# Re-ordering three row-square additions and one small product in a hand-scheduled graph-network kernel

## Chip, cores and metric

The kernel runs on one core of a Trainium2 chip (trn2). The metric is device time in microseconds (us) for the whole launch: median, lowest and highest of three runs. One further execution was taken with the hardware profiler; all durations quoted from "the trace" come from that one. Engines are named as the profile names them: PE (TensorE; PEld is its weight load), DVE (VectorE), ACT (ScalarE), POOL (GpSimd), SP (the engine whose queue issues the DMAs).

## What is computed

Sixteen graphs (batches) of 1024 nodes with 128 features each and a dense weighted adjacency matrix `adj` of 1024 x 1024 float32 values. Cut to what matters, the reference is:

```python
def gnn0(x, adj):                       # first block
    deg = adj.sum(-1)[:, :, None]
    s = einsum('bid,bij->bjd', x, adj) / deg
    return relu(concat([x, s], -1) @ W.T + b)

def layer(nodes, adj):                  # second block, four of these
    src = nodes @ ws + bs
    src_agg = einsum('bjv,bij->biv', src, adj / l2norm_of_rows(adj))
    dst = nodes @ wd + bd
    dst_agg = einsum('bjv,bji->biv', dst, adj / l2norm_of_columns(adj))
    own = nodes @ wn + bn
    return tanh(concat([src_agg, own, dst_agg], 2) @ wu + bu)

x = layernorm(x + gnn0(x, adj))
x = layernorm(x + four_layers(x, adj))  # layers 2 and 3 also take earlier outputs as input
```

The two norms of `adj` need, for each batch, the sum of the squares of every row and of every column. Those sums, and one of the two layer norms, are what the change touches.

## The kernel before

**Tiling.** One pass of the loop `for b in range(B)` does the four layers (0 to 3) of batch b and, in between, everything that batch n = b + 1 needs before its own layers: loading `adj`, its row and column norms, scaling, the first block, and its layer norm. `a` is batch b's matrix scaled by columns (128 partitions, 8 blocks of 1024), `at` its transpose scaled by rows. `a2` (`w["a"]` while it is fresh) is the matrix of batch n. The second norm of batch b - 1 is finished during layers 1 and 2 of batch b.

**Matrix products.** Each layer's aggregation is a Strassen-like scheme of seven products of half-size blocks, for each of the two directions (DST, with `a`; SRC, with `at`). It needs sums of quarters of the matrices: `T` for `a` and `Q` for `at`; `combine(i, y, T)` (lines 674 to 682) writes quarter sum i with one DVE instruction over 128 x 2048 elements. Every product has 64 output rows, so PE works on two at once, an "upper" one on output partitions 64 to 127 and a "lower" one on 0 to 63. `aggregate` lists the upper and lower products; `in_turn` interleaves them and numbers the upper ones. One such *step* is one upper and one lower product of 64 x 512, which the trace shows as two PE records each.

**What sets the order.** Nothing is left to a scheduler: all engines run exactly in the order in which the Python code issues. `aggregate` carries two dictionaries from step number to function. `events` are the layer's own reads of finished products, `hooks` are other work to be issued ahead of that step; at one step, events come first. PE's instructions of a hook therefore stand in PE's queue at that step, while DVE's and ACT's instructions just join their own queues at that place.

**Layer 0, steps and reads (batches 1 to 15).** Upper: Z1, Z0 own terms (steps 0, 1), M1 DST (2 to 5), M2 DST (6 to 9), M1 SRC (10 to 13), Z21 DST (14 to 17), M2 SRC (18 to 21, reads `Q[2]`), M3 SRC (22 to 25, reads `Q[3]`), Z21 SRC (26 to 29, reads `Q[4]`). The reads that matter here:

- before step 14, `m1_read` (L884, L885): two ACT copies;
- before step 22, `m2_and_half_of_m3`: DVE add L892, ACT copy L893, DVE add L910; then `m4_read`: ACT copies L888, L889;
- before step 26, `last_reads`: DVE adds L896 (the read of M3) and L901, ACT copy L897, DVE add L902, then the tanh L1018 on ACT that writes the upper half (columns 512 to 1023) of `f1T`;
- after the last step: DVE add L1007 (`e0 + Z0`) and the tanh L1018 of the other half of `f1T`.

Layer 1 then begins with `messages` (L247 products `pt`, which read `f1T`: first the upper half, 16 PE records, then the lower half, 16 more), whose results DVE adds at L698, followed by the sums L710 to L713.

**Row and column squares of batch n.** `squares_of_row(n, a, st, i)` is an ACT Square of row block i into a tile `sq` (line 322), which also yields the row sums. `add_squares` adds those tiles up on DVE into `acc`: line 329 for the first pair, line 331 for the others. The `sq` tiles come from a pool of two buffers, so the Square of row block 2 waits until the first addition has freed a buffer. Row blocks 0 to 3 are done in layer 0, 4 to 7 in layer 1; then `column_sums` (L339, L344) reduces `acc`, and `inverses` (L368 to L376) ends with a power of -1/2 on POOL (L376). These hooks exist in the passes b = 1 to 14; b = 0 has its own arrangement, and b = 15 has no next batch.

**The norm in layer 1.** `begin1` (step 2), `centre1` (16), `squares1` (19) and `rstd1` form the second layer norm of batch b - 1. `squares1` is the DVE reduction L446, which writes `v`. `rstd1` calls `norm_rstd`: a product of `v` with a constant matrix on PE (L252, tile `pv`, four small records), a DVE scaling of it (L454, tile `ve`) and a power on POOL (L456, tile `rs`). `norm_end` (L461) uses `rs` in layer 2.

The hooks before the change, layer 0 first:

```python
hooks = {0: rows3, 3: weights1, 5: lambda: combine_1(yt), 7: lambda: combine(2, yt, Q),
         9: lambda: combine(3, yt, Q), 11: lambda: combine(4, yt, Q), 15: sums1, 20: additions(1),
         22: additions(then=(2, 3)), 27: additions(2, 3)}
...
hooks = alongside(sums_of_next, {2: begin1, 16: centre1, 19: squares1, 23: rstd1})
```

`additions(*which, then)` issues the DVE additions of `which` and then the ACT Squares of `then`; `sums1` issues the Squares of row blocks 0 and 1.

Of the kernel before, what the change touches and what calls it, by code (L numbers as in the profile page):

```python
# [23 lines left out]
def adj_resnorm_kernel(ctx: ExitStack, tc: tile.TileContext, x, adj, w0, b0, layers, out):  # L24
# [308 lines left out]
    def column_sums(b, state):  # L333

        column_reduce(b, state, column_transpose(b, state))
# [326 lines left out]
    def quarters(a):  # L662
        return {(j, h): a[:, j * NJ:(j + 1) * NJ, half(h)] for j in range(2) for h in range(NH)}
# [4 lines left out]
    def combined(b, kind):  # L668

        return {i: one.tile([P, NJ, HW], F32, tag=f"{kind}{i}", name=f"{kind}{i}_{b}") for i in (2, 3, 4)}  # L670
# [5 lines left out]
    def combine(i, y, T):  # L676
        if i == 2:
            nc.vector.tensor_sub(T[2], y[1, 1], y[0, 1])  # L678
        elif i == 3:
            nc.vector.tensor_sub(T[3], T[2], y[0, 0])  # L680
        else:
            nc.vector.tensor_sub(T[4], y[1, 0], T[2])
# [342 lines left out]
    def alongside(hooks, more):  # L1025

        def both(i):
            def run():
                hooks[i]()
                more[i]()  # L1030
            return run

        return hooks | {i: both(i) if i in hooks else f for i, f in more.items()}
# [36 lines left out]
    Q = combined(0, "Q")  # L1070
# [166 lines left out]
    for b in range(B):  # L1237
        nxt = b + 1 < B
        n = b + 1
        y, yt = quarters(a), quarters_t(at)  # L1240
# [5 lines left out]
        if b == 0:  # L1246
            def row_factors0():
                nonlocal rinv
                rinv = gather_inverses(0, row_inverses(0, inv))
                column_sums(0, st0)  # L1250
                for q in (2, 3):
                    scale_rows(rows[q], q, rinv)

            t = messages(b, 0, feats, wm, {0: lambda: to_x1(0), 2: row_factors0}, with_sums=False)
            cinv = {}

            def columns0(rows, h, engine=nc.vector):
                scale_columns(a, cinv[0], rows, half(h), engine)

            def rows0(destination, finish):  # L1260
                for q in (2, 3):
                    transpose_rows(rows[q], q, at)

            def cinv0(destination, finish):
                cinv[0] = factor_rows_now(0, 1, inv, "cinv")

            def second0(destination, finish):
                columns0(range(NJ, NB), 1)
                sums_of_weights(2, fetched[2][3])
                weight_sums(own_seven(2, fetched[2][3]))  # L1270
                nc.sync.dma_start(wsave[2], fetched[2][3])
                destination(1, cinv[0])
                columns0(range(NJ), 1)

            def fold_and_scale(l, q):
                fold_begin(l, fetched[l])
                scale_rows(rows[q], q, rinv)

            def first0(destination, finish):
                columns0(range(NJ, NB), 0, nc.gpsimd)  # L1280
                columns0(range(2), 0, nc.gpsimd)
                for q in (0, 1):
                    transpose_rows(rows[q], q, at)
                destination(0, cinv[0])
                columns0(range(2, NJ), 0)

            def sums0(destination, finish):
                combine_1(y)
                finish(1)
                combine(2, y, T)  # L1290
                combine_1(yt)
                combine(3, y, T)

            def folded(l, part):
                return lambda *_: part(l, fetched[l])

            hooks = {4: lambda *_: inverses(0, st0, NB), 5: folded(2, fold_begin), 6: rows0, 7: cinv0,
                     8: folded(2, fold_end), 9: lambda *_: fold_and_scale(3, 0), 11: second0, 12: folded(3, fold_end),
                     14: lambda *_: scale_rows(rows[1], 1, rinv), 18: first0, 26: sums0}
            T = combined(0, "T")  # L1300
            plain_layer(b, 0, feats, t, wm, a, at, f1, "acc", hooks)
            wm = message_weights(b, 1)
            a2 = load(n)
            xs2 = load_spread(n)
        else:
            w = {}
            if nxt:
                st = begin_sums(n)
            t = messages(b, 0, feats, wm)
            if nxt:  # L1310
                w["a"] = load(n)
            Q = combined(b, "Q")
            ahead = {}

            def weights1(ahead=ahead):
                combine(4, y, T)
                ahead["wm"] = message_weights(b, 1)

            def rows3():
                transpose_rows(rows[0], 0, at)  # L1320

            def sums1(w=w, st=st):
                if nxt:
                    for i in range(2):
                        squares_of_row(n, w["a"], st, i)

            def additions(*which, then=(), w=w, st=st):
                def issue():
                    if nxt:
                        for i in which:  # L1330
                            add_squares(n, st, i)
                        for i in then:
                            squares_of_row(n, w["a"], st, i)
                return issue

            hooks = {0: rows3, 3: weights1, 5: lambda: combine_1(yt), 7: lambda: combine(2, yt, Q),
                     9: lambda: combine(3, yt, Q), 11: lambda: combine(4, yt, Q), 15: sums1, 20: additions(1),
                     22: additions(then=(2, 3)), 27: additions(2, 3)}
            aggregate(b, 0, feats, t, wm, a, at, T, Q, f1, "row", hooks)
            wm = ahead["wm"]  # L1340
            a2, xs2 = w.get("a"), None
# [21 lines left out]
        hooks = {}  # L1363
        if b == 0:
            hooks = {0: sums_of(0, 1, add=(1,)), 1: lambda: combine(2, yt, Q), 2: sums_of(of=FIRST),
                     3: sums_of(2, 3, add=(2, 3)), 4: lambda: combine(3, yt, Q), 5: sums_of(4, 5, add=(4, 5)),
                     6: lambda: combine(4, y, T), 13: sums_of(6, 7), 18: lambda: combine(4, yt, Q), 19: sums_of(of=LAST),
                     22: sums_of(add=(6, 7)), 27: lambda: column_sums(n, st)}
            st = begin_sums(n)
        else:  # L1370
            nm = f"1_{b - 1}"
            w = {"ys": summed(f"y{nm}", "xa")}
            sums_of_next = {}
            if nxt:
                sums_of_next = {0: sums_of(4, 5), 1: sums_of(of=FIRST, add=(4, 5)), 2: sums_of(6, 7),
                                8: sums_of(add=(6, 7)), 9: lambda: column_sums(n, st), 15: sums_of(of=(4,)),
                                18: sums_of(of=(5,)), 20: lambda: inverses(n, st), 21: sums_of(of=(6,)),
                                24: sums_of(of=(7,))}

            def begin1(w=w, nm=nm):  # L1380
                norm_spread(w["ys"], f4, KS)
                w["s"] = norm_sum(w["ys"], KS, nm, back)

            def centre1(w=w, nm=nm):
                w["sq"] = norm_centre(w["ys"], w["s"], KS, nm)
                if nxt:
                    w["xs"] = load_spread(n)

            def squares1(w=w, nm=nm):
                w["v"] = norm_squares(w["sq"], KS, nm)  # L1390

            def rstd1(w=w, nm=nm):
                w["r"] = norm_rstd(w["v"], KS, nm)

            hooks = alongside(sums_of_next, {2: begin1, 16: centre1, 19: squares1, 23: rstd1})
        hooks = alongside(hooks, {3: weights2})
        p = {}

# [6 lines left out]
        hooks = alongside(hooks, {11: y4, 27: t2})  # L1405
# [49 lines left out]
        hooks, between = {4: end1} if b else {}, {}  # L1455
        if nxt:
            scales = [lambda: scale(0, 1), lambda: scale(NJ, 1), lambda: scale(0, 0), lambda: scale(NJ, 0)]
            if b == 0:
                between = {1: inverses3, 2: factors}
                hooks = {1: load_xn, 5: factors_of_rows, 7: start3, 18: factors_gathered,  # L1460
                         **dict(zip((10, 12, 14, 16), scales))}
                quarters_at = (20, 22, 25)
            else:
                between = {0: factors, 3: end1_and_load}
                hooks = {2: factors_of_rows, **dict(zip((4, 5, 7, 9), scales)), 10: factors_gathered, 16: start3}
# [8 lines left out]
        hooks = alongside(hooks, {23: weights3})  # L1474
        if b == 0:
            hooks = alongside(hooks, {8: lambda: weight_sums(own_seven(3, None))})
# [9 lines left out]
        hooks, between = {}, {}  # L1486
        if nxt:
# [75 lines left out]
            def rows3():  # L1563
# [4 lines left out]
            hooks = {5: rstd0, 7: rows0, 11: quarter0, 15: end0, 8: scale2, 16: scale3, 18: acc_rows, 22: rows1, 23: lambda: scale1(0),  # L1568
                     26: lambda: scale1(1), 27: rows2, 30: rows3}
        else:  # L1570
# [17 lines left out]
            hooks = {30: residual_last, 31: transpose_last}  # L1588
# [66 lines left out]
```

## Time and profile before

| what | value |
|---|---|
| three runs: median (lowest to highest) | 2426.66 us (2425.36 to 2427.37) |
| profiled execution: its own time | 2427.01 us |
| profiled execution: span, first to last instruction | 2425.1 us |
| PE busy | 2384.9 us (98% of the span) |
| DVE busy | 2084.5 us (86%) |
| ACT busy | 977.2 us (40%) |
| POOL busy | 273.5 us (11%) |
| mean granted TensorE clock | 0.998 |
| column-square additions, L329 and L331 together | 105, of 1.22 us each |
| Squares, L322 | 120, of 1.05 us each |

How to read it: the busy share of an engine says how much of the span it had an instruction running. PE matmuls are pipelined and their ends are modelled, so a matmul record of 0.59 us does not mean that PE spends 0.59 us on it; the distance from one start to the next does. A number in square brackets behind a record of the timeline is the idle time of that engine just before it, with the instruction that ended the wait.

### The profile page before, as it was taken

What the parts mean: (1) busy time and instruction counts of PE and PEld (TensorE: products, weight loads), DVE (VectorE), ACT (ScalarE), POOL (GpSimd) and SP (SyncE); (2) the same over time, 40 slices, a digit from 0 to 9 for tenths busy, and PEclk for the clock granted to TensorE, in tenths of its full rate; (3) what the DMA queues carried; (4) which work ended last, traced back from release to release, by engine and by line L of the source; (5) the groups of instructions that cost most, each with busy time, mean ns of one, the idle gap of its engine ahead of it and who ended that gap; (6) DMA issues with size and microseconds to landing.
All of it is one profiled execution on the core that took longest, in us unless ns stands there. A gap on an engine that the chain in (4) does not pass through costs nothing.

```text
span 2425.1 us, 39279 instructions
## 1 busy us (share of the span) xinstructions
PE 2384.9 (98%) x15293; PEld 1213.7 (50%) x15293; DVE 2084.5 (86%) x2799; ACT 977.2 (40%) x1827; POOL 273.5 (11%) x102
## 2 busy tenths in 40 slices
PE   8999999999999999999999999999999999999998
PEld 4444464544645446454554545546454464544644
DVE  5998888988889889889888889888898888988954
ACT  5524344253343524435244452434425334253312
POOL 4101111001111011110111100111100111101100
PEclk9999999999999999999999999999999999999999
DMA  9527244262633627235272442634427253362400
GB/s 205 120 74 145 68 116 86 71 143 56 138 71 82 135 48 160 56 96 114 54 162 52 110 96 66 150 68 105 87 70 154 56 128 79 73 142 50 99 21 21
DMA packets 365896, 232.02 MB, mean 96 GB/s; under 512 B 152784, under 2 KB 336848, under 8 KB 365712
## 3 DMA queue, kind: packets, MB, share of 16 engines
q1 hardware_dynamic: 364944, 227.16, 42.1%
q0 software_dynamic: 768, 2.36, 0.4%
q8 instruction: 121, 1.98, 0.3%
q14 instruction: 63, 0.52, 0.1%
HBM read 209.59 MB, written 19.84 MB: 95 GB/s over the span
## 4 chain that ended last, share of the span: by engine, by line
PE 55%; DVE 26%; ACT 7%; SPq 4%; DMA 4%; issue 4%; DVEq 0%; POOLq 0%; ACTq 0%
PE m L1005 20%; PE z L1005 13%; PE pt L247 6%; PE pt_z L247 5%; PE m_f L583 5%; SPq L640 4%; DVE acc L331 3%; PE z_f L583 2%; PE pw L247 2%; DVE at L655 2%; DVE t L698 2%; DMA rows<-in_adj_dram 2%; ACT a L647 2%; DVE Q L678 1%; DVE Q L680 1%
## 5 line engine op out<-in xcount | busy, mean ns | idle before, releaser
L1005 PE MATMUL m<-a,t 128*64 128x512 f32 x1008 | 432.3, 593 | 0.2 <-DVE t L711 0.2
L1005 PE MATMUL m<-at,t 128*64 128x512 f32 x1008 | 417.0, 592 | 0.0
L1005 PE MATMUL m<-Q,S 128*64 128x512 f32 x880 | 394.0, 593 | 0.0
L1005 PE MATMUL m<-T,S 128*64 128x512 f32 (+1 forms) x1040 | 393.1, 573 | 0.0
L456 POOL TENSOR_TENSOR rs<-ve,mhalf 128x32 f32<-128x32 f32 x30 | 191.6, 6385 | 996.1 <-DVE ve L454 996.1
L1005 PE MATMUL z<-at,t 128*64 128x512 f32 x504 | 232.0, 593 | 0.0
L1005 PE MATMUL z<-at,S 128*64 128x512 f32 x504 | 228.3, 593 | 0.0
L1005 PE MATMUL z<-a,S 128*64 128x512 f32 x504 | 228.2, 593 | 0.0
L1005 PE MATMUL z<-a,t 128*64 128x512 f32 x504 | 226.8, 592 | 0.0
L1005 PE MATMUL z<-Q,t 128*64 128x512 f32 x504 | 226.6, 592 | 0.0
L1005 PEld LDWEIGHTS m<-T,S 128*64 128x64 f32 x1040 | 133.6, 137 | 127.0 <-issue 123.5
L1005 PEld LDWEIGHTS m<-a,t 128*64 128x64 f32 x1008 | 133.2, 137 | 123.9 <-issue 114.0
L1005 PEld LDWEIGHTS m<-at,t 128*64 128x64 f32 x1008 | 134.9, 137 | 113.2 <-issue 110.8
L1005 PEld LDWEIGHTS m<-Q,S 128*64 128x64 f32 x880 | 118.2, 137 | 114.8 <-issue 112.9
L1005 PE MATMUL z<-T,t 128*64 128x512 f32 x384 | 175.7, 593 | 0.0
L884 ACT COPY e<-m 64x512 f32<-64x512 f32 x63 | 36.6, 581 | 335.4 <-PE m L1005 334.9
L376 POOL TENSOR_TENSOR inv<-cols,mhalf 128x16 f32<-128x16 f32 (+1 forms) x17 | 46.8, 2752 | 1050.4 <-DVE cols L375 1050.4
L414 DVE TENSOR_TENSOR a<-a,cinv 128x512 f32<-128x512 f32 x250 | 154.1, 692 | 1.4 <-ACT cinv L351 1.3
L247 PE MATMUL pt<-wm,f1T 128*64 128x128 f32 (+1 forms) x1536 | 124.7, 310 | 14.6 <-ACT f1T L1018 14.6
L322 ACT ACTIVATE sq<-a 128x1024 f32<-128x1024 f32 x120 | 125.8, 1049 | 14.4 <-DVE acc L331 13.4
L247 PEld LDWEIGHTS pt<-wm,f1T 128*64 128x64 f32 x1536 | 94.3, 137 | 63.4 <-ACT f1T L1018 32.2
L317 ACT ACTIVATE a<-a 128x1024 f32<-128x1024 f32 x120 | 125.3, 1045 | 0.4
(300 smaller groups left out, 4922.3 us busy)
## 6 DMA issues: line engine op xcount, KB each, us to landing
a<-in_adj_dram SPq DMA_DIRECT2D x120, 512.0 KB, 12.9
rows<-in_adj_dram SPq DMA_DIRECT2D x480, 64.0 KB, 2.1
a<-in_adj_dram SPq DMA_DIRECT2D x240, 128.0 KB, 3.4
wm<-wsave SPq DMA_DIRECT2D x32, 704.0 KB, 5.3
wm<-wsave SPq DMA_DIRECT2D x31, 320.0 KB, 3.1
xn<-in_x_dram SPq DMA_DIRECT2D x124, 64.0 KB, 5.4
xs<-in_x_dram SPq DMA_DIRECT2D x60, 128.0 KB, 3.6
cinv<-dr SPq DMA_DIRECT2D x30, 256.0 KB, 6.3
```

The costliest lines, as they stand in the source:

```text
L247: nc.tensor.matmul(out[s], x[:, s], y, start=start, stop=stop)
L317: nc.scalar.activation(a[:, i, :], a[:, i, :], AF.Copy, accum_out=degree)
L322: nc.scalar.activation(sq, a[:, i, :], AF.Square, accum_out=state["cols"][:, i:i + 1])
L331: nc.vector.tensor_add(state["acc"], state["acc"], state[i])
L414: engine.tensor_mul(a[:, i, s], a[:, i, s], cinv[:, s])
L456: nc.gpsimd.tensor_tensor(rstd, ve, mhalf[:, :n], ALU.pow)
L583: nc.tensor.matmul(o, x_, y_, start=start, stop=stop)
L640: nc.sync.dma_start(piece[g * C:(g + 1) * C, :, h * P:(h + 1) * P], v[h, g, :, k:k + n])
L647: nc.scalar.activation(row, row, AF.Copy, scale=rinv[:, q * QB + k:q * QB + k + 1])
L655: nc.vector.transpose(at[h][:, j:j + NJ, c].rearrange("p j (k c) -> p j k c", c=C), piece.rearrange("p k (j c) -> p j k c", c=C)[:, j:j + NJ])
L698: nc.vector.tensor_add(t[j][:, o:o + 2].rearrange("p k a v c -> p k (a v c)"), pt, wm[:, 0][:, None, :].to_broadcast([P, 2, 2 * P]))
L1005: nc.tensor.matmul(o, x, y_, start=start, stop=stop)
```

## The change

Only two dictionaries of hooks change. In layer 0 of passes 1 to 14, the first addition of squares is issued at step 16 instead of 20, and the quarter sum `Q[4]` at step 17 instead of 11, so that the addition stands ahead of `Q[4]` in DVE's queue. The Squares of row blocks 2 and 3 are issued at step 18 instead of 22. The addition of row block 2 is issued at step 23 instead of 27; that of row block 3 stays at 27. In layer 1, `rstd1` is issued at step 26 instead of 23 (passes 1 to 15).

```diff
             hooks = {0: rows3, 3: weights1, 5: lambda: combine_1(yt), 7: lambda: combine(2, yt, Q),
-                     9: lambda: combine(3, yt, Q), 11: lambda: combine(4, yt, Q), 15: sums1, 20: additions(1),
-                     22: additions(then=(2, 3)), 27: additions(2, 3)}
+                     9: lambda: combine(3, yt, Q), 15: sums1, 16: additions(1), 17: lambda: combine(4, yt, Q),
+                     18: additions(then=(2, 3)), 23: additions(2), 27: additions(3)}
...
-            hooks = alongside(sums_of_next, {2: begin1, 16: centre1, 19: squares1, 23: rstd1})
+            hooks = alongside(sums_of_next, {2: begin1, 16: centre1, 19: squares1, 26: rstd1})
```

In the order of each engine this gives, for one of those passes: DVE runs L680 (`Q[3]`), L329, L682 (`Q[4]`), L892, L910, L331, L896, L901, L902, L331, L1007, where it ran L680, L682, L329, L892, L910, L896, L901, L902, L331, L331, L1007. ACT runs the four Squares in a row ahead of L893, L888, L889, where the last two Squares stood behind L889. On PE the four small records of `pv` move three steps back. No instruction is added or removed, and the orders on SP and POOL stay the same.

## The prediction, as put on record

> **What bounds the kernel now.** I read the page's busy shares first, then PE's own waits, then the timeline of one pass (b = 2; the others repeat it), then that of the last pass (b = 15).
>
> ```profile
> PE 2384.9 (98%) x15293; PEld 1213.7 (50%) x15293; DVE 2084.5 (86%) x2799; ACT 977.2 (40%) x1827; POOL 273.5 (11%) x102
> ```
>
> PE is the bound, so only a change in PE's idle time can move the end. Who makes PE wait (total us, times, longest):
>
> ```profile
> PE pt L247 <- ACT f1T L1018: 14.6, 14, 1.0
> PE pv L252 <- DVE v L446: 6.9, 14, 0.5
> ```
>
> Two waits recur 14 times, once in each pass that prepares a next batch, and they are the two places that the edit touches. The first, in pass 2:
>
> ```profile
> 377.90 0.69 DVE L910 TENSOR_TENSOR e<-e,e 64x512 f32<-64x512 f32 x1 [0.68 <-ACT e L893]
> 379.78 0.69 DVE L896 TENSOR_TENSOR e<-e,m 64x512 f32<-64x512 f32 x1 [1.19 <-PE m L1005]
> 381.30 0.61 ACT L897 COPY e<-e 64x512 f32<-64x512 f32 x1
> 381.94 0.69 DVE L902 TENSOR_TENSOR e<-e 128x512 f32<-128x512 f32 x1 [0.75 <-ACT e L897]
> 382.55 2.48 DVE L331 TENSOR_TENSOR acc<-acc,sq 128x1024 f32<-128x1024 f32 x2
> 382.67 0.72 ACT L1018 ACTIVATE f1T<-e,bout 128x512 f32<-128x512 f32 x1 [0.76 <-DVE e L902]
> 382.99 0.59 PE L1005 MATMUL z<-at,t 128*64 128x512 f32 x1
> 383.44 1.95 PE L247 MATMUL pt<-wm,f1T 128*64 128x256 f32 x16
> 384.95 0.68 DVE L1007 TENSOR_TENSOR e<-e,z 128x512 f32<-128x512 f32 x1
> 385.66 0.72 ACT L1018 ACTIVATE f1T<-e,bout 128x512 f32<-128x512 f32 x1 [2.27 <-DVE e L1007]
> 386.44 1.95 PE L247 MATMUL pt<-wm,f1T 128*64 128x256 f32 x16 [1.04 <-ACT f1T L1018]
> 388.21 1.03 PE L1005 MATMUL z<-f1T,wm 128*64 128x512 f32 x4
> ```
>
> PE's last product of layer 0 starts at 382.99 and would release L1007 some 0.6 later, but two additions hold DVE until 384.95; L1007, the tanh and the second half of the messages are late by that much. Just before, DVE idles 0.68, 1.19 and 0.75: room for the additions. Pass 15 has no additions and shows the place without them:
>
> ```profile
> 2313.91 0.59 PE L1005 MATMUL z<-at,t 128*64 128x512 f32 x1
> 2313.93 4.06 PE L247 MATMUL pt<-wm,f1T 128*64 128x256 f32 x32
> 2314.54 0.69 DVE L1007 TENSOR_TENSOR e<-e,z 128x512 f32<-128x512 f32 x1 [1.64 <-PE z L1005]
> 2317.82 1.03 PE L1005 MATMUL z<-f1T,wm 128*64 128x512 f32 x4
> ```
>
> The second wait, in layer 1 of pass 2: the small product stands in PE's queue before its operand `v` is there.
>
> ```profile
> 407.48 1.22 DVE L446 TENSOR_REDUCE v<-sq 128x32 f32<-128x1024 f32 x1
> 407.76 0.59 PE L1005 MATMUL z<-T,t 128*64 128x512 f32 x1
> 408.85 0.31 PE L252 MATMUL pv<-v,fold 128*64 128x32 f32 x4 [0.49 <-DVE v L446]
> 408.96 0.62 PE L1005 MATMUL z<-T,t 128*64 128x512 f32 x1
> 411.54 0.18 DVE L454 TENSOR_SCALAR ve<-pv 128x32 f32<-128x32 f32 x1
> ```
>
> [...]L1007 starts at 384.95, right behind the additions, though its operand was ready near 383.6. [...]So I count PE from start to start: a pair of 64 x 512 records takes 0.43 (407.33 to 407.76), not 0.59. [...]in pass 15 the messages start 0.02 after the last lower product, on the free half.
>
> **Part 1, layer 0.** One addition is 1.22 (rows L329, L331), a quarter sum 2.2, a Square 1.05, all moved and none added. Worked through pass 2:
>
> - DVE ends `Q[3]` at 373.16. Squares 0 and 1 are done by 372.8, so the first addition runs 373.16 to 374.4 and `Q[4]` ends at 376.5 instead of 375.3. PE wants `Q[4]` at step 26, 379.58: hidden, 3.0 spare. L892 starts at 376.52 as before.
> - ACT: Squares 2 and 3 get their buffers at 374.4 and run to 376.6 (2 x 1.05 and a 0.19 accumulator read), inside ACT's idle 4.45 ahead of L893. L893 (377.25), L888 and L889 are not delayed. Their rows came with the same four transfers as rows 0 and 1, squared from 370.6 on. Nothing else moves on ACT; SP and POOL have nothing moved past them.
> - Addition 2 follows L910: 378.6 to 379.83, in the 1.19 idle. L896 moves from 379.78 to 379.85: 0.07.
> - L897 no longer stands behind two Squares (it waited until 381.30): it starts at 380.6, when L896 is done. L902 runs 381.2 to 381.9, and the upper `f1T` half is there at 382.65 instead of 383.39. PE can start the messages at 383.01 instead of 383.44.
> - Addition 3: 381.9 to 383.15. L1007 then waits for PE alone: in pass 15 it starts 0.63 after the last product, here 382.99 + 0.63 = 383.62, with 0.45 spare.
>
> From the last product's start to layer 1's own terms, pass 2 takes 388.21 - 382.99 = 5.22 and pass 15 takes 2317.82 - 2313.91 = 3.91. I take the whole difference, **1.31 per pass**; the 1.04 that PE's waits give is the lower end (it counts modelled ends and leaves out the 0.43 at 383.44). What remains of a wait, about 0.35, is the chain L1007, tanh, messages, which pass 15 has too.
>
> DVE behind L1007 follows PE's messages (L698 idled 0.74 for PE), so all of layer 1 comes 1.31 earlier on DVE, ACT and PE alike, `v` included. This part alone would leave the second wait at its size.
>
> **Part 2, layer 1.** From product to product across `pv`, pass 2 takes 408.96 - 407.76 = 1.20; pass 15, where `v` was early, takes 0.52. So the wait is **0.68** (lower end 0.49, the waits' number). Three steps are 3 x 2 x 0.43 = 2.57 of PE work; the wait is covered with about 1.9 spare. The four small records cost the same 0.1 anywhere. Who waits for them now: on DVE L454, ahead of L721. Without the stall step 26 falls at 408.96 - 0.68 - 0.1 + 2.57 = 410.75 in the old frame, `pv` is there at about 411.05, and L454 came at 411.54: still no wait, 0.5 spare; beyond that, L1007 there idled 2.05 for PE. On POOL, L456 starts at 412.39 anyway, because it queues behind L376; L461 reads its result at 427.42. If that cover were gone, each us of delay of L721 beyond 2.05 would hit the messages of layer 2.
>
> **Sum.** 14 x (1.31 + 0.68) = 27.9 us. Against the profiled execution's own 2427.01 (span 2425.1 and 1.9 around it), that is 2399.1; this execution lies 0.35 above the median, so the runs should show about **2399**. With both lower ends, 14 x 1.53 = 21.4: 2405. Next in line is PE itself: the remaining gaps in pass 2 are below 0.1 each but for the 0.35.
>
> **Rivals.**
>
> - *The addition at M3's read becomes the wait.* If addition 2 could only start when M3 is ready (379.78), L896 starts at 381.0, the upper half of `f1T` comes at 383.8, L1007 at 384.4 and the second messages at 385.86 instead of 386.44: gain 0.58 + 0.68, times 14 = 17.6: **2409**. For it: the slots fit within 0.07, and addition 2 needs Square 2. Against: Square 2 is ready 3 us earlier. Chance 0.12.
> - *The small product's wait only changes place*, to L454 and L721 or to layer 2's messages: only 14 x 1.31 = 18.3: **2408**. Against it: the 2.05 that DVE idles at L1007. Chance 0.10.
> - *Slower: the Squares stall ACT ahead of the reads.* If rows 2 and 3 landed only with the last of the eight transfers of the next matrix (the last is issued at 359.5 and lands 19.9 us later, 379.4), Square 2 would start at 379.4 instead of 374.4, L893 at 381.5, and the chain L910, addition 2, L896, L897, L902 would bring the messages' second half to about 388.8: 2.4 later than now, less 0.68, so 14 x 1.7 = 24 us: **2451**. It turns into a loss once Square 2 starts after about 377.7, 3.3 later than I expect. Against it: rows 0 and 1, of the same transfers, are squared at 370.6 without a wait. Chance 0.04.
> - *No change*: the gains are given back at a place that the trace doesn't show as tight. Chance 0.02. That the change doesn't do what it says is excluded by the orders on the engines, which are written out by hand.
>
> **Numbers.** The forecast, 2396 to 2405 by itself, has 0.72. Faster: 0.72 + 0.12 + 0.10 = 0.94; within 0.2% (4.9 us, about what a measurement here tells from no change) 0.02; slower 0.04. The range reaches to 2409 to take in the first two rivals; its low end is the forecast less 3 us for the spread of single executions and for some of the 0.35.
>
> **What would show it.** In the profile after: both rows gone or near zero among PE's waits (I allow 0.3 per pass at the second messages); one addition between L910 and L896 and one ahead of L1007, the latter starting about 0.63 after the last product; 3.9 from that product to layer 1's own terms; L897 right behind L896; `pv` without idle before it. The forecast is wrong if L896 starts well behind M3's end, if ACT idles before Square 2 for a DMA, or if L454 or L721 waits for `pv`.

## The result, and the profile after

| | before | after |
|---|---|---|
| median (lowest to highest), four runs each | 2426.93 us (2425.36 to 2427.37) | 2397.44 us (2397.09 to 2398.95) |
| profiled execution: own time, span | 2427.01, 2425.1 us | 2397.22, 2395.3 us |
| one pass (median distance from one layer 0's last product to the next) | 148.51 us | 146.48 us |
| last product of layer 0 to layer 1's own terms (pass 2) | 5.22 us | 3.91 us |
| product to product across `pv` (pass 2) | 1.20 us | 0.51 us |

The ratio is 0.9881, with a 95% interval of 0.9864 to 0.9898: 1.2% faster. The forecast was 2399.

The page's busy line and the line of the chain that ended last, by engine, of the kernel after:

```profile
PE 2377.4 (99%) x15293; PEld 1195.3 (50%) x15293; DVE 2088.5 (87%) x2799; ACT 977.2 (41%) x1827; POOL 273.8 (11%) x102
...
PE 95%; DVE 2%; DMA 1%; SPq 1%; issue 0%; ACT 0%; POOLq 0%; DVEq 0%; ACTq 0%
```

The same chain line of the kernel before:

```profile
PE 55%; DVE 26%; ACT 7%; SPq 4%; DMA 4%; issue 4%; DVEq 0%; POOLq 0%; ACTq 0%
```

PE's own busy time fell by 7.5 us only, the span by 29.8: the other 22.3 us were idle time of PE. The chain tells it best. Before, two short waits per pass were enough to lead the walk back from PE into the DVE queue for a quarter of the span; after, it hardly leaves PE. The three longest waits that PE still has:

```profile
PE w0tr L1099 <- POOL ident masks.py:199: 4.3, 1, 4.3
PE pa L1127 <- issue: 2.1, 1, 2.1
PE pt L247 <- DVE e L721: 1.2, 1, 1.2
```

All three occur once; the rows with a count of 14 are gone. Pass 2 around the end of layer 0, kernel after (start, duration, engine, line; in brackets the idle time before and what ended it):

```profile
370.89 1.06 ACT L322 ACTIVATE sq<-a 128x1024 f32<-128x1024 f32 x1 [1.50 <-DVE acc L329]
...
373.81 0.62 ACT L893 COPY e<-e 64x512 f32<-64x512 f32 x1 [0.74 <-DVE e L892]
...
375.18 1.23 DVE L331 TENSOR_TENSOR acc<-acc,sq 128x1024 f32<-128x1024 f32 x1
...
376.44 0.69 DVE L896 TENSOR_TENSOR e<-e,m 64x512 f32<-64x512 f32 x1
...
377.16 0.61 ACT L897 COPY e<-e 64x512 f32<-64x512 f32 x1 [1.54 <-DVE e L896]
...
378.56 1.22 DVE L331 TENSOR_TENSOR acc<-acc,sq 128x1024 f32<-128x1024 f32 x1
...
379.55 0.59 PE L1005 MATMUL z<-at,t 128*64 128x512 f32 x1
379.60 4.03 PE L247 MATMUL pt<-wm,f1T 128*64 128x256 f32 x32
380.18 0.69 DVE L1007 TENSOR_TENSOR e<-e,z 128x512 f32<-128x512 f32 x1 [0.40 <-PE z L1005]
380.91 0.72 ACT L1018 ACTIVATE f1T<-e,bout 128x512 f32<-128x512 f32 x1 [1.51 <-DVE e L1007]
...
383.46 1.89 PE L1005 MATMUL z<-f1T,wm 128*64 128x512 f32 x8
```

The two Squares run inside ACT's idle time; one addition fills the slot ahead of L896, one ends before PE's last product does; L1007 now idles 0.40 *for PE*, where before PE idled for it. L1007 starts 0.63 behind the product, as pass 15 of the kernel before had it. And across the small product of layer 1:

```profile
402.73 1.22 DVE L446 TENSOR_REDUCE v<-sq 128x32 f32<-128x1024 f32 x1
...
405.58 0.59 PE L1005 MATMUL z<-T,t 128*64 128x512 f32 x1
...
406.01 0.26 PE L252 MATMUL pv<-v,fold 128*64 128x32 f32 x4
406.10 0.62 PE L1005 MATMUL z<-Q,t 128*64 128x512 f32 x1
...
406.79 0.18 DVE L454 TENSOR_SCALAR ve<-pv 128x32 f32<-128x32 f32 x1
...
407.64 5.43 POOL L456 TENSOR_TENSOR rs<-ve,mhalf 128x32 f32<-128x32 f32 x1
```

`v` is ready at 403.95, 2.06 ahead of `pv`; L454 takes its place on DVE without an idle note, and L456 starts right behind L376 (404.78 + 2.90), as it did before.

### The profile page after: what moved, and what is told of

Read it like the earlier page. It is cut to its first block, busy times and chain, and to the rows that moved or that the text cites. A ratio compares the mean times of both kernels' runs of the same rounds, so it can differ in the third digit from the quotient of the medians.

```text
span 2395.3 us, 39279 instructions
## 1 busy us (share of the span) xinstructions
PE 2377.4 (99%) x15293; PEld 1195.3 (50%) x15293; DVE 2088.5 (87%) x2799; ACT 977.2 (41%) x1827; POOL 273.8 (11%) x102
## 4 chain that ended last, share of the span: by engine, by line
PE 95%; DVE 2%; DMA 1%; SPq 1%; issue 0%; ACT 0%; POOLq 0%; DVEq 0%; ACTq 0%
PE m L1005 39%; PE z L1005 29%; PE pt L247 9%; PE m_f L583 5%; PE pt_z L247 5%; PE z_f L583 2%; PE pw L247 2%; PE m3s L1005 1%; PE z L851 1%; DMA wm<-in_L_gnn_ws_dram 1%; PE pt_p L247 1%; SPq L640 0%; DVE acc L331 0%; DMA raw<-in_L_gnn_wu_dram 0%; DMA a<-in_adj_dram 0%
## 5 line engine op out<-in xcount | busy, mean ns | idle before, releaser
L456 POOL TENSOR_TENSOR rs<-ve,mhalf 128x32 f32<-128x32 f32 x30 | 191.9, 6395 | 987.9 <-DVE ve L454 987.9
L376 POOL TENSOR_TENSOR inv<-cols,mhalf 128x16 f32<-128x16 f32 (+1 forms) x17 | 46.8, 2751 | 1031.9 <-DVE cols L375 1031.9
L247 PEld LDWEIGHTS pt<-wm,f1T 128*64 128x64 f32 x1536 | 100.0, 137 | 39.2 <-issue 18.7
```

The source lines that it names most:

```text
L247: nc.tensor.matmul(out[s], x[:, s], y, start=start, stop=stop)
L376: nc.gpsimd.tensor_tensor(inv[:, s], cols[:, s], mhalf[:, s], ALU.pow)
L456: nc.gpsimd.tensor_tensor(rstd, ve, mhalf[:, :n], ALU.pow)
```

## The experiments

The theory: PE is the bound and has two separate waits per pass, each caused by the order in a queue; each is worth its start-to-start excess over pass 15, 1.31 and 0.68, in 14 passes. The rivals, besides those of the prediction: the first wait passes on into the second; the gain is the Squares' doing alone or the additions' doing alone; the order of `Q[4]` or of the landings does not matter. Kernels e1 to e4 were measured together (the kernel before beside them: 2424.97 us), and so were e5 to e8 (2425.73). Because sessions and executions differ by one or two us, the finest comparison is the one by pass, from the traces: "stretch" is last product of layer 0 to the first of layer 1's own terms, "across pv" the distance from product to product there.

| kernel | us, median (lowest to highest) | ratio to before (95%) | pass | stretch | across pv |
|---|---|---|---|---|---|
| e1 layer 0 part alone | 2407.34 (2406.61 to 2408.85) | 0.9929 (0.9913 to 0.9946) | 147.18 | 3.90 | 1.19 |
| e2 norm part alone | 2415.51 (2414.45 to 2418.13) | 0.9962 (0.9948 to 0.9977) | 147.80 | 5.23 | 0.51 |
| e3 additions at 27 | 2406.14 (2405.58 to 2407.81) | 0.9923 (0.9909 to 0.9938) | 147.17 | 4.60 | 0.51 |
| e4 Squares at 22 | 2413.71 (2412.25 to 2415.02) | 0.9953 (0.9938 to 0.9968) | 147.63 | 5.06 | 0.51 |
| e5 `Q[4]` first | 2411.83 (2410.28 to 2412.66) | 0.9943 (0.9928 to 0.9958) | 147.47 | 4.90 | 0.51 |
| e6 row blocks 4 and 5 | 2462.80 (2457.45 to 2469.59) | 1.0155 (1.0136 to 1.0174) | 151.64 | 6.5 to 11.0 | 0.51 |
| e7 norm at 24 | 2397.58 (2396.19 to 2398.24) | 0.9884 (0.9869 to 0.9899) | 146.48 | 3.90 | 0.51 |
| e8 last tanh in two pieces | 2395.98 (2395.36 to 2397.29) | 0.9877 (0.9861 to 0.9894) | 146.44 | 3.43 | see text |

### e1 and e2: each part alone

```diff
-            hooks = alongside(sums_of_next, {2: begin1, 16: centre1, 19: squares1, 26: rstd1})
+            hooks = alongside(sums_of_next, {2: begin1, 16: centre1, 19: squares1, 23: rstd1})
```

> The layer-0 part alone; rstd1 goes back to step 23. Own theory (two separate waits of PE): from the last product of layer 0 to layer 1's own terms 3.91 as in the changed kernel (5.22 before), and the wait of pv keeps its 0.68, since v comes earlier by the same amount as PE; a pass takes 147.2 instead of 148.51, total about 2408.6 us. Rival (the first wait passes into the second): PE meets pv earlier by 1.31 while v doesn't move, pv waits about 2.0, and the total stays near 2427. Rival (the layer-0 part also cures pv): near 2398.

> The norm part alone: the hooks of layer 0 as before, rstd1 at step 26. Own theory: the gap across pv falls from 1.20 to 0.52, layer 0 keeps its 5.22, a pass takes 147.8, total about 2417.4 us. Rival (the wait only changes place, to L454 and L721): total within 2 us of 2427. A third question is the opening: the changed kernel's profiled run was some 1.4 us ahead before the first changed hook; if that is chance, the two parts' gains by passes (18.3 + 9.5) sum to the whole without it.

e2 is the kernel before with `rstd1` at 26. A pass gains 148.51 - 147.18 = 1.33 in e1 and 148.51 - 147.80 = 0.71 in e2, together 2.04; the whole change gains 2.03. The parts add up, and neither feeds on the other. PE's longest wait in e1:

```profile
PE pv L252 <- DVE v L446: 6.8, 14, 0.5
```

and in e2:

```profile
PE pt L247 <- ACT f1T L1018: 14.6, 14, 1.0
```

Each kernel keeps exactly the row that its part leaves alone, at its old size. That the first wait passes into the second is out: in e1 `v` moved forward together with PE.

### e3, e4, e5: the three orders inside the layer 0 part

e3 puts the addition of row block 2 back beside that of block 3:

```diff
-                     18: additions(then=(2, 3)), 23: additions(2), 27: additions(3)}
+                     18: additions(then=(2, 3)), 27: additions(2, 3)}
```

> The changed kernel, but the addition of row block 2 goes back to step 27, beside that of row block 3; the Squares stay early. Own theory: L897 and L902 keep their early places, but two additions stand ahead of L1007, which starts about 1.34 after the last product instead of 0.63; the stretch to layer 1's own terms is 4.6 instead of 3.91, a pass takes 147.2, total about 2407 us. Rival (the gain comes from the Squares leaving L897, the additions' place matters little): 2397.4.

```profile
378.72 2.47 DVE L331 TENSOR_TENSOR acc<-acc,sq 128x1024 f32<-128x1024 f32 x2
381.11 0.68 DVE L1007 TENSOR_TENSOR e<-e,z 128x512 f32<-128x512 f32 x1
```

L1007 follows the pair without idle time, 1.33 behind the last product, and 0.70 of the 1.31 is lost. The early Squares, with the first addition ahead of `Q[4]`, are worth the rest, 5.22 - 4.60 = 0.62.

e4 leaves the additions where the change has them and puts the Squares back behind L889:

```diff
-                     18: additions(then=(2, 3)), 23: additions(2), 27: additions(3)}
+                     22: additions(then=(2, 3)), 23: additions(2), 27: additions(3)}
```

> The changed kernel, but the Squares of row blocks 2 and 3 go back to step 22, behind L889. Own theory: the addition at step 23 now waits for Square 2 (done about 1.5 later than L910), so that L896, L897, L902 and L1007 all come late: the stretch from the last product to layer 1's own terms is about 5.05, a pass takes 147.6, total about 2413 us. Rival (only the additions' places count): 2397.4. If the waiting addition were worse than this (the slower rival's mechanism), above 2420.

```profile
376.04 1.06 ACT L322 ACTIVATE sq<-a 128x1024 f32<-128x1024 f32 x1
...
377.22 1.23 DVE L331 TENSOR_TENSOR acc<-acc,sq 128x1024 f32<-128x1024 f32 x1 [1.68 <-ACT sq L322]
378.48 0.69 DVE L896 TENSOR_TENSOR e<-e,m 64x512 f32<-64x512 f32 x1
```

The addition waits 1.68 for its Square and L896 stands behind it: this is the first rival of the prediction, made to happen. Only 0.16 of the 1.31 is left.

e5 puts `Q[4]` back ahead of the first addition, and the Squares, which need the buffers that this addition frees, behind it:

```diff
-                     9: lambda: combine(3, yt, Q), 15: sums1, 16: additions(1), 17: lambda: combine(4, yt, Q),
-                     18: additions(then=(2, 3)), 23: additions(2), 27: additions(3)}
+                     9: lambda: combine(3, yt, Q), 11: lambda: combine(4, yt, Q), 15: sums1,
+                     20: additions(1, then=(2, 3)), 23: additions(2), 27: additions(3)}
```

> The changed kernel, but Q4 goes back to step 11 and so ahead of the first addition; the first addition and the Squares of row blocks 2 and 3 are issued at step 20, still ahead of layer 0's reads. Own theory: the first addition ends 2.2 later, so the Squares run 376.5 to 378.7 in the old frame and delay L893 by 1.5, and with it L910, the addition behind it and L896; the stretch from the last product to layer 1's own terms is about 4.95, a pass takes 147.5, total about 2412 us. Rival (Q4's place is of no account): 2397.4.

```profile
372.08 1.22 DVE L329 TENSOR_TENSOR acc<-sq,sq 128x1024 f32<-128x1024 f32 x1
...
376.19 0.69 DVE L910 TENSOR_TENSOR e<-e,e 64x512 f32<-64x512 f32 x1 [2.17 <-ACT e L893]
```

L910 waits 2.17 for L893, which stands behind the late Squares (0.68 in the kernel after). Of the 1.31, 0.32 is left. So the three moves are not three gains: with the addition of row block 2 back in its old place (e3) about half of the 1.31 is gone, with either of the others back (e4, e5) three quarters of it or more. `Q[4]` moved in order to let the first addition free two buffers early; that frees the Squares; those free the addition at M3's read and the copy L897.

### e6: the slower rival, made true

Layer 0 squares and adds row blocks 4 and 5, layer 1 then 2 and 3:

```diff
-                     18: additions(then=(2, 3)), 23: additions(2), 27: additions(3)}
+                     18: additions(then=(4, 5)), 23: additions(4), 27: additions(5)}
...
-                sums_of_next = {0: sums_of(4, 5), 1: sums_of(of=FIRST, add=(4, 5)), 2: sums_of(6, 7),
+                sums_of_next = {0: sums_of(2, 3), 1: sums_of(of=FIRST, add=(2, 3)), 2: sums_of(6, 7),
```

> The changed kernel, but layer 0 squares and adds row blocks 4 and 5 in place of 2 and 3, which change places with them in layer 1; the amount of work is the same. Their rows come with the last four of the eight transfers. It makes the slower rival of the prediction come true: the Square waits on ACT, ahead of L893, for the last landing (about 379.4 in the old frame). Own theory: the stretch from the last product to layer 1's own terms grows to about 7.6, total about 2449 us. Rival (the order of landing does not matter): 2397.4.

```profile
380.82 1.06 ACT L322 ACTIVATE sq<-a 128x1024 f32<-128x1024 f32 x1 [6.63 <-DMA a<-in_adj_dram]
```

The Square waits 6.63 for the transfer, L893 stands behind it, and the mechanism is the one expected. The size is not: 65 us above the kernel after instead of 52. The windows of pass 2 (stretch in us, its length, then busy time and instructions of PE, PEld, DVE, ACT and POOL, then the granted TensorE clock; the last two are DMA) show why:

```profile
375.00:384.00 9.00, 9.00 (x46) 3.88 (x43) 3.87 (x4) 3.13 (x6) 0.00 (x0) 1.00 0.51 107
384.00:388.00 4.00, 0.94 (x5) 0.06 (x1) 3.80 (x6) 1.55 (x4) 0.00 (x0) 0.88 0.00 0
388.00:391.00 3.00, 2.33 (x12) 1.38 (x14) 1.90 (x3) 1.99 (x3) 0.00 (x0) 0.50 0.00 0
391.00:394.00 3.00, 3.00 (x18) 1.67 (x16) 1.08 (x2) 3.00 (x7) 0.00 (x0) 0.52 0.02 5
394.00:397.00 3.00, 3.00 (x22) 1.38 (x19) 2.68 (x5) 2.59 (x6) 0.00 (x0) 1.00 0.00 0
```

PE stands idle from about 384.8 to 388.7, and the clock is at half from 387.0, still within this gap, to 393.9. The 32 message records take 6.05 us; at the full clock they take 3.51. Passes 5, 6 and 14 of this run kept the full clock, and their stretches are 7.62, 7.08 and 6.47, against 7.6 expected. In the other eleven passes the messages take 4.8 to 6.4 us, together 22 us more than at the full clock. The passes differ as much as they do (6.5 to 11.0) by this and by how late the rows land: the first message starts 3.0 to 4.9 behind the last product.

The length of the wait alone does not say which pass loses the clock. Here are the first messages of pass 5, which kept the full clock, and of pass 10, which lost it:

```profile
846.43 0.87 PE L247 MATMUL pt<-wm,f1T 128*64 128x256 f32 x6 [3.52 <-ACT f1T L1018]
...
1601.94 3.48 PE L247 MATMUL pt<-wm,f1T 128*64 128x256 f32 x16 [2.37 <-ACT f1T L1018]
```

The shorter wait, 2.37, is the one with the low clock: its 16 messages take 3.48, against 1.95 for 16 in pass 2 of the kernel before, at a clock of 1.00. What tells the two passes apart was not shown. In the traces of the kernels before and after, the clock stays at 1.00 through passes 1 to 15 up to the last 5 us of the span (to 2420.3 of 2425.1 and to 2391.0 of 2395.3). The mean clock of the profiled execution is 0.988 in e6 and 0.998 to 1.0 in all the others.

### e7: how much of the norm's move is needed

```diff
-            hooks = alongside(sums_of_next, {2: begin1, 16: centre1, 19: squares1, 26: rstd1})
+            hooks = alongside(sums_of_next, {2: begin1, 16: centre1, 19: squares1, 24: rstd1})
```

> The changed kernel with rstd1 at step 24 instead of 26. Own theory: one step is 0.86 of PE's work and the wait was 0.68, so one step already covers it, with 0.18 to spare: total 2397.4, pv without idle before it. Rival (v comes later by some tenths in the new order, or the wait is more than the trace shows): pv waits again, up to 0.7 per pass, total up to 2407.

A pass takes 146.48, as with step 26, and PE doesn't wait for `v`. One step (0.86 of PE's work) covers 0.68; the other two are reserve.

### e8: the last tanh of layer 0 in two pieces

```diff
-        if pieces == 1:
+        if l == 0:
+            for k in range(0, BPH, 2):
+                z, o = nodes(e0)[:, :, k:k + 2], blocks(fT[:, half(0)])[:, :, k:k + 2]
+                nc.vector.tensor_add(z, z, nodes(Z0)[:, :, k:k + 2])
+                nc.scalar.activation(o, z, AF.Tanh, bias=bout[l])
+        elif pieces == 1:
             nc.vector.tensor_add(e0, e0, Z0)
             squash(l, 0, e0, fT)
```

> The changed kernel with the last add and tanh of layer 0 (L1007 and the tanh behind it) split in two pieces of 256 columns, in the order in which the messages read them, in passes 1 to 15. Own theory (what is left of PE's wait is the chain L1007, tanh, messages): the first piece is there 0.63 + 0.42 + 0.45 and two hand-overs, about 1.6, after the last product starts, before PE is through with the first 16 records (1.77), so the stretch to layer 1's own terms falls from 3.91 to about 3.56; 15 x 0.35 = 5 us, total about 2392 us. Rival (the rest of the gap belongs to PE's change of shape): 3.91 stays, total 2397.4 or a little more for the added instructions.

The stretch shrinks as expected, even a little more (3.43), yet a pass is only 0.04 shorter, 0.6 us in fifteen instead of the 5 expected. Against e7, measured beside it, the total is 1.6 us lower with overlapping ranges: a version that would clearly beat the kernel after this is not. Where the 0.35 went shows in PE's timeline of pass 2 of this kernel:

```profile
380.65 0.59 PE L1005 MATMUL z<-at,t 128*64 128x512 f32 x1
380.84 3.42 PE L247 MATMUL pt<-wm,f1T 128*64 128x256 f32 x29
384.08 0.59 PE L1005 MATMUL z<-f1T,wm 128*64 128x512 f32 x1
384.10 0.59 PE L247 MATMUL pt<-wm,f1T 128*64 128x256 f32 x2
384.51 1.47 PE L1005 MATMUL z<-f1T,wm 128*64 128x512 f32 x6
```

PE's upper and lower products run as two streams (in this trace their records start 0.02 apart, at 388.37 and 388.39, and each stream's next one 0.43 later), and at the end of layer 0 the upper one is about a record (0.38 in the kernel after, 0.45 here) ahead of the other. In the kernel after, only this leading stream waits for the second tanh: its ninth message record starts 0.35 late, while the lagging stream goes from 381.493 to 381.709, its regular 0.216. Taking that wait away lets the leading stream begin its own terms at 384.08, but the lagging one still has message records at 384.10 and begins at 384.53, 3.88 behind the last product (3.91 in the kernel after).

Counted from the last product of layer 0, the leading stream then runs 0.47 earlier than in the kernel after through all of layer 1, and the lagging one 0.03. At `pv` nothing is lost: each stream takes 0.52 from product to product there in both kernels, and 0.94 from the leading stream's last product before to the lagging one's first behind is only the distance between the two. The lead ends in the messages of layer 2. There the leading stream has no record from 413.63 to 414.01, since the product next in turn reads the `e` that L763 on DVE writes from 413.18 to 413.86; meanwhile the lagging stream catches up.

## Why the prediction was right, by its steps

- **PE is the bound, and only its idle time moves the end.** Right: 14 x 2.03 = 28.4 of the 29.8 us between the two profiled executions arise in the 14 changed passes.
- **Part 1, 1.31 per pass, from pass 15.** Right: 1.33 in e1. The lower end of 1.04, the sum of PE's noted waits, was too low. The noted waits start at a modelled end and leave out the upper half's delay; counting from start to start was worth 4 us of forecast in this part.
- **Its steps.** L896 delayed by 0.07: right in kind, it stands directly behind the addition; against the last product it is 0.10 later than before. L897 right behind L896, L1007 0.63 behind the last product: right (0.40 of spare where 0.45 was forecast). `Q[4]` hidden: right, PE has no wait at step 26.
- **Part 2, 0.68.** Right: 0.71 in e2. L454 and L721 without a new wait, L456 behind L376: right.
- **"What remains of a wait, about 0.35."** Right as a length on one stream, wrong as a reserve (the prediction put some of it into the low end of its range): removing it gained 0.04 per pass (e8), since the lagging stream did not wait there.
- **The sum.** 2399.1 forecast for the profiled execution, 2397.2 measured. Of the 1.9, 0.6 is 14 x (2.03 - 1.99). The other 1.4 lies in the opening, ahead of anything that was changed, and is not the change's doing (by the passes alone the gain is 28.4, against 27.9 forecast): the last product of layer 0 in pass 1 starts at 234.48 in the trace before and at 233.08 in the one after. It is a low clock in the kernel before. Both traces begin the same 16 products at 13.3, but in the one before they take 8.80 us and in the one after 7.10; in the same 3.4 us PE has six records against ten, at a clock of 0.51 against 1.00 (in each pair the kernel before stands first):

```profile
13.32 8.80 PE L1127 MATMUL pa<-a,xn 128*128 128x512 f32 x16 [2.81 <-issue]
13.31 7.10 PE L1127 MATMUL pa<-a,xn 128*128 128x512 f32 x16 [2.10 <-issue]
...
13.90:17.30 3.40, 3.40 (x6) 1.34 (x5) 2.44 (x3) 2.28 (x5) 1.73 (x1) 0.51 1.04 318
13.90:17.30 3.40, 3.40 (x10) 1.48 (x9) 2.44 (x3) 2.28 (x5) 1.73 (x1) 1.00 1.04 318
```

Of the ten traces, those of the kernel before and of e8 come latest to that product of pass 1, at 234.5 and 234.2; the others come at 232.2 to 233.3. The waits before these 16 products differ from trace to trace as well (noted at 1.2 in e4, at 2.8 in the kernel before); what varies them was not tried.

- **The rivals.** The first is what e4 does, at a price of 1.15 per pass of part 1 (the prediction had 0.73: it let the addition start when M3 is ready, and Square 2, behind L889, comes half a us later still). The second, that the small product's wait only changes place, is out: e2 gained 0.71 per pass. The slower one has its place and mechanism right and its price too low, 24 us against 37 (2462.80 - 2425.73), mostly because the clock's drop was left out: of the 42.6 us that separate the two profiled executions, 22 are the messages' extra time at the low clock.

## What to carry to other kernels

Price a wait of a busy PE from start to start, against a pass in which the suspected work is absent, and not by the noted idle time. In an engine that runs its queue in order, as DVE does here (behind two additions, L1007 starts 1.33 after the last product in e3, against 0.63), look for the last instruction before a releasing one that could run earlier, then for what *that* one waits for (here a buffer, freed by an addition, held up by an unrelated sum): the whole chain has to move, and moving two links of three bought a tenth to a half of the gain. With two streams on PE, ask which of them waits: here a wait of the leading one alone was no loss, because the lagging one set the pace. A reorder that leaves PE idle can cost more than the gap itself: in eleven passes of e6 the clock dropped as well, and their messages took 22 us more than at the full clock.

## What the runs showed that was not expected

- The length of a gap alone did not decide the clock: in e6 the pass with a noted wait of 2.37 us lost the full clock and the one with 3.52 did not. What told the two apart was not shown. Where it dropped, the 32 messages took 1.3 to 2.9 us longer. In the kernel before, waits of 1.04 us (at 386.44) and 1.22 us (at 116.43) left it at 1.00.
- A wait of 0.35 on the leading one of PE's two streams cost almost nothing: without it a pass was 0.04 shorter (e8).
- In pass 2 the power on POOL over 128 x 32 values takes 5.43 us in one norm and 7.34 in the other, in both kernels (spans on POOL are rough in this profile).
